# Turned rows of a graph-attention stack: seven steps of waiting instead of four, their copies on ScalarE, and one tile of a block's closing work per step

## The chip, the cores and the metric

The kernel runs on one core of a Trainium2 chip, in one launch. The metric is the device time of one execution in microseconds (us), lower is better. A core has engines that each work through their own stream of instructions: TensorE (PE) multiplies matrices, VectorE (DVE) and ScalarE (ACT) work elementwise, GpSimd (POOL) does little here, SyncE (SP) issues the DMA transfers of this kernel. A semaphore makes an instruction wait for the work of another engine or for a DMA.

## The reference, cut to what matters

Four layers run over one graph of N = 3327 nodes with 256 features and a mask `adj` (N x N). Each ends in a residual sum and a layer norm. The first is a cosine attention, the second a graph-attention (GAT) layer, the third a query-key attention. The fourth, layer 3 of the code, is where the change acts. It has a matrix product ahead and then three GAT layers one behind the other:

```python
def _gat_layer(h, adj, W, a):
    Wh = h @ W
    f1 = Wh @ a[:F_out]
    f2 = Wh @ a[F_out:]
    e = leaky_relu(f1 + f2.T, ALPHA)
    att = where(adj > 0, e, NEG_INF)
    att = softmax(att, axis=1)
    return elu(att @ Wh)
h = input @ W0
h = _gat_layer(h, adj, W1, a1)
h = _gat_layer(h, adj, W2, a2)
h = _gat_layer(h, adj, W3, a3)
...
x = _layernorm(x + h)
```

All is float32. Nearly all the arithmetic is in the products `att @ Wh`, one per layer, 3327 x 3327 by 3327 x 256.

## The kernel before

**Tiles, blocks, steps.** The nodes are padded to 26 tiles of 128. The rows of the result are worked on in seven blocks of 512 rows (four tiles), the last one, block 6, of 256. There are six layers in the code, "0", "1", "2", "3a", "3b" and "3c"; the last three are the GAT layers of layer 3, and `deep(L)` is true for them. One list of steps `(L, b, j)` runs over layers, blocks and the 26 tiles `j` of the sum. In each step the loop makes attention weights some steps ahead, issues the matmuls of the step, and then calls `advance()` once.

**Weights.** For a tile, `Gat.weights` lets ScalarE write `re` (L787) into one of four buffers and VectorE multiply it with the mask into `ft` (L800). In the deep layers two pairs of tiles are then combined on VectorE by `quad_sums` (L871 to L874), or one pair by `sums` (L883 to L886), since products go pair by pair in a Strassen form of seven products: 13 pairs a block. A pair has 14 matmuls (L935), each of them two records in the profile. The other operand of the form, sums of rows of `v`, is written to memory once by `combine` (L843 to L853) and fetched for each block and pair by `fetch_tsum` (L857, `tsums`). Blocks 0 to 5 use this form, block 6 the plain one (L1644; in 3c a form of its own, L1610).

**Closing a block.** When the last pair of a block is done, its sums stand in PSUM, and `finish(L, b, pos)` has to turn them into rows of the next layer. It is a generator: each `advance()` carries it from one `yield` to the next, so that it is spread over the steps of the next block. In the deep layers it does this: `joined` adds up the seven products (L961 to L979); `normed` divides by the row sums (L1175, L1177); `turn` transposes the four tiles; `projected` multiplies a tile with the layer's weights (L1230, `pproj`), and ScalarE takes `exp` and `relu` of it (L1239, L1242); `activated` joins these into `v` (L1254); `follow` adds to the sum of rows (L1084) and to the scores of the next layer (L719); `combine` follows each second tile. In 3c a layer norm and the store of the result follow instead.

**Turning.** `turn` lets ScalarE split the rows into their low and high 16-bit halves (`planes`, L990), issues one DMA transpose on SP (L993), waits `steps` yields, and copies the two halves from `turned` into `pT` on VectorE (L1000). How many yields it waits is said by `turn_steps` (L1003): four, but in block 5 (`NB - 2`) seven, and nine in 3c. In block 5 `finish` also yields after each `activated`.

**Order.** SP's queue holds, besides the transposes, the fetches of `tsums`, the mask of the next block (1664 KB, issued in step 8), the stores of `combine` and the rows of scores. What is left of a closing at step 22 of a block is carried out there at once. A scheduler then places the instructions of each engine, so an instruction can stand elsewhere in its engine's stream than the step in which it was issued.

Of the kernel before, what the change touches and what calls it, by code (L numbers as in the profile page):

```python
# [33 lines left out]
def gnn_stack(ctx: ExitStack, tc: tile.TileContext, a: dict, N: int, out: bass.AP):  # L34
# [8 lines left out]
    nc = tc.nc  # L43
    NT = (N + P - 1) // P
    NP = NT * P
    NB = (NP + CH - 1) // CH
# [36 lines left out]
    n = 8  # L83
# [738 lines left out]
    def deep(L):  # L822
        return L.i > 2
# [6 lines left out]
    def combine(key, p, v, e=None):  # L830


        b1, b2 = v[2 * p], v[2 * p + 1]
        b11, b12, b21, b22 = b1[:, H:D], b1[:, :H], b2[:, H:D], b2[:, :H]
        if (key, p) in kept or key == "0":
            t = work.tile([P, 4 * H + 1], F32, tag="tsum", name="tsums", bufs=3)
        else:
            t = work.tile([P, 4 * H + 1], F32, tag="x4k", name="tsum", bufs=2)
        if (key, p) in kept:
            tsums[kept[key, p], p] = t  # L840
        t1, t2, t3, t4 = (t[:, c : c + H] for c in (0, H + 1, 2 * H + 1, 3 * H + 1))
        if e is None:
            nc.gpsimd.memset(t[:, H : H + 1], 1.0)  # L843
            nc.vector.tensor_tensor(t1, b12, b11, ALU.subtract)
            nc.vector.tensor_tensor(t3, b22, b12, ALU.subtract)
        else:
            one = t[:, H : H + 1]
            nc.vector.tensor_scalar(one, e[:, :1], 0.0, None, ALU.is_ge)
            nc.vector.scalar_tensor_tensor(t1, b12, one, b11, ALU.mult, ALU.subtract)
            nc.vector.scalar_tensor_tensor(t3, b22, one, b12, ALU.mult, ALU.subtract)  # L850
        nc.vector.tensor_tensor(t2, b22, t1, ALU.subtract)
        nc.vector.tensor_tensor(t4, t2, b21, ALU.subtract)
        nc.sync.dma_start(t_d[key][p], t)  # L853
# [126 lines left out]
        return z[:, : 2 * q]  # L980


    def turn(x4, n, out, steps=3):

        half = "p k (n t) -> p t k n"
        pl = work.tile([P, 4, 2, D], U16, tag="x4k", name="planes", bufs=2)
        for t in range(2):
            nc.scalar.copy(pl[:, :n, t, :], x4[:, :n, :].bitcast(U16).rearrange(half, t=2)[:, t])  # L990
        yield
        tr = work.tile([P, 16, P], U16, tag="stage", name="turned", bufs=4)
        nc.sync.dma_start_transpose(  # L993
            out=tr[:, : 4 * n, :], in_=pl[:, :n].rearrange("p k t n -> p (k t n)")
        )
        for _ in range(steps):
            yield
        trv = tr[:, : 4 * n, :].rearrange("p (k t h) i -> p t k h i", t=2, h=2)
        for t in range(2):
            nc.vector.tensor_copy(out(t), trv[:, t])  # L1000
        yield

    def turn_steps(L, b):  # L1003

        if L.key == "1":
            return 5 if b == NB - 2 else 3
        return (9 if L.key == "3c" else 7) if b == NB - 2 else 4

# [82 lines left out]
    def finish(L, b, pos):  # L1093
# [4 lines left out]
        n = len(ts_)  # L1098
# [71 lines left out]
        else:  # L1170
# [23 lines left out]
            if L.key in x_d:  # L1194
                x4 = work.tile([P, 4, D], F32, tag="stage", name="x4", bufs=4)
# [8 lines left out]
            if L.key != "2":  # L1204
                pT4 = work.tile([P, 4, 2, P], F32, tag="x4k", name="pT4", bufs=2)
                yield from turn(
                    p4,
                    n,
                    lambda t: pT4[:, :n].bitcast(U16).rearrange(
                        "p k h (i t) -> p t k h i", t=2  # L1210
                    )[:, t],
                    turn_steps(L, b),
                )
                pTs = {k: pT4[:, k] for k in range(n)}
                if L.key == "1" and b < NB - 2:
                    c4 = work.tile([P, 4, D], F32, tag="x4k", name="c4", bufs=2)
                    yield from projected4(pT4, w[L.w], c4)

            def projected(k):


                if L.key == "2":
                    src = p4[:, k, :]
                elif L.key == "1" and b < NB - 2:
                    src = c4[:, k, :]
                else:
                    pm = bank("pproj")
                    pT = pTs.pop(k)
                    for h in range(2):
                        nc.tensor.matmul(  # L1230
                            pm[:, :D],
                            pT[:, h, :],
                            w[L.w][:, h, :],
                            start=(h == 0),
                            stop=(h == 1),
                        )
                    src = pm[:, :D]
                e = work.tile([P, D], F32, tag="elu_e", name="elu_e", bufs=2)
                nc.scalar.activation(e, src, AF.Exp)  # L1239
                if L.hidden:  # L1240
                    y = work.tile([P, D], F32, tag="y", name="z", bufs=6)
                    nc.scalar.activation(y, src, AF.Relu)  # L1242
                else:
                    y = work.tile([P, D], F32, tag="y", name="y", bufs=6)
                    nc.vector.scalar_tensor_tensor(
                        y, src, 0.0, xr[k], ALU.max, ALU.add
                    )
                es[k] = e
                ys.append(y)

            def activated(k):
                e, y = es.pop(k), ys[k]
                x = nxt[ts_[k]][:, :D] if L.hidden else y
                nc.vector.scalar_tensor_tensor(x, e, 1.0, y, ALU.min, ALU.add)  # L1254
                if L.hidden:
                    follow([k], {k: x})
                else:
                    stats(k)

            for p in range(n + 2):  # L1260
                if p >= 2:
                    activated(p - 2)
                    if b == NB - 2:
                        yield
                    if L.hidden and p % 2 and b < NB - 1:
                        combine(layers[L.i + 1].key, (ts_[0] + p - 3) // 2, nxt)
                if 1 <= p <= n:
                    projected(p - 1)
                if p > 0:
                    yield  # L1270
        if not L.hidden:
# [29 lines left out]
            if L.key == "1":  # L1301
                yield from turn(
                    o4,
                    n,
                    lambda t: FT[b].bitcast(U16).rearrange(
                        "p h (k i t) -> p t k h i", k=4, t=2
                    )[:, t, :n],
                    4 if b == NB - 2 else 3,
                )
                for k, t in enumerate(ts_):  # L1310
                    pm = bank("pv")
                    for h in range(2):
                        nc.tensor.matmul(
                            pm[:, :D],
                            FT[b][:, h, k * P : (k + 1) * P],
                            w["v"][:, h, :],
                            start=(h == 0),
                            stop=(h == 1),
                        )
                    nc.vector.tensor_tensor(nxt[t][:, :D], pm[:, :D], w["bv"], ALU.add)  # L1320
                    if k % 2:
                        yield
                        if b < NB - 1:
                            combine("2", t // 2, nxt)
                dsts = [nxt[t][:, :D] for t in ts_]
# [146 lines left out]
    steps = [(L, b, j) for L in layers for b in range(NB) for j in range(NT)]  # L1472
# [79 lines left out]
    for s, (L, b, j) in enumerate(steps):  # L1552
# [146 lines left out]
        if j == NT - 1:  # L1699
            if b == 0 and not last:  # L1700
                nl = layers[L.i + 1]
                L.sum = Sum()
                if nl.is_gat:
                    if nl.key == "1":
                        while "row_1" not in w:
                            next(setup)
                    nl.gat = Gat(nl.key)
                    L.gat_next = nl.gat
            if end:
                pending.append(finish_last(pos[1:], xm, 1))  # L1710
            else:
                pending.append(finish(L, b, pos))
            advance()
# [65 lines left out]
```

## Time and profile before

| | before |
|---|---|
| median of 3 runs | 2300.66 us (2299.2 to 2301.87) |
| the profiled execution | 2297.41 us |
| its span in the profile | 2295.6 us |
| its mean granted TensorE clock | 0.996 |
| TensorE busy | 2257.2 us (98%) |
| VectorE busy | 1998.3 us (87%) |
| ScalarE busy | 1210.3 us (53%) |
| layer 3, from about 1370 us | some 926 us of the span |

The profile is one execution as the hardware recorded it. The busy rows give each engine's share of the span; the waits view lists, for each group of waiting instructions, the engine, the operation and its line, what released it, then the total in us, the number of times and the longest; the timeline lists instructions or runs of them in order of time, with start and duration, and in brackets the idle time ahead and what ended it. In a group's line `x54` is a number of instructions and `449/738/757` the least, mean and largest duration in ns.

### The profile page before, as it was taken

How to read it: one execution, taken by the hardware profiler on the slowest of the kernel's cores; microseconds unless marked ns; L12 is line 12 of the kernel's file. 1: busy time of each engine (PE TensorE's matmuls, PEld its weight loads, DVE VectorE, ACT ScalarE, POOL GpSimd, SP SyncE). 2: the span in 40 equal slices, each digit the busy share in tenths (PEclk: the TensorE clock that was granted, in tenths of full speed). 3: DMA queues.
4: the chain of work that ended last, by engine and by line, in shares of the span. 5: the costliest groups of instructions: out<-in, count | busy, mean ns of one | idle time of the engine just before them, and what ended most of it. 6: DMA issues, size and time to landing. Idle time of an engine off the chain costs nothing. (4 is left out here: it accounts for less than half of the span.)

```text
span 2295.6 us, 41529 instructions
## 1 busy us (share of the span) xinstructions
PE 2257.2 (98%) x15183; PEld 2004.7 (87%) x15183; DVE 1998.3 (87%) x5437; ACT 1210.3 (53%) x1982; POOL 49.4 (2%) x196
## 2 busy tenths in 40 slices
PE   9999999999999999999999999999999999999997
PEld 7788888888888877888888899999999999999997
DVE  7789999866777777898898889999899999899996
ACT  4667777764555423223223246555666555655653
POOL 0000001000000000000000000000000000000000
PEclk9999999999999999999999999999999999999999
DMA  8655565523222322132132254444444445355542
GB/s 281 192 178 179 186 195 187 161 84 89 78 72 55 105 61 81 56 100 81 56 99 71 74 171 130 133 136 143 124 129 137 131 134 148 98 152 169 149 122 58
DMA packets 186207, 286.13 MB, mean 125 GB/s; under 512 B 80413, under 2 KB 105492, under 8 KB 181396
## 3 DMA queue, kind: packets, MB, share of 16 engines
q1 hardware_dynamic: 185732, 283.22, 41.2%
q8 instruction: 120, 1.97, 0.4%
q14 instruction: 83, 0.68, 0.1%
q10 hardware_dynamic: 272, 0.26, 0.0%
HBM read 228.21 MB, written 38.44 MB: 116 GB/s over the span
## 5 line engine op out<-in xcount | busy, mean ns | idle before, releaser
L787 ACT ACTIVATE re<-u,nrh,th 128x512 f32<-128x512 f32 (+1 forms) x728 | 539.8, 778 | 343.0 <-DVE ft L800 179.7
L1644 PE MATMUL po<-v,e 128*128 128x257 f32 x1872 | 422.3, 381 | 0.9 <-ACT p L1177 0.8
L1644 PEld LDWEIGHTS po<-v,e 128*128 128x128 f32 x1872 | 352.6, 190 | 60.9 <-issue 9.8
L935 PE MATMUL po<-tsums,qsum 128*128 128x128 f32 (+1 forms) x2520 | 352.8, 275 | 1.4 <-DMA tsums<-t3b_d 0.7
L800 DVE SCALAR_TENSOR_TENSOR ft<-re,rh,mask 128x512 f32<-128x512 f32 x468 | 341.1, 747 | 2.6 <-ACT re L787 2.6
L935 PEld LDWEIGHTS po<-tsums,qsum 128*128 128x128 f32 x2520 | 316.2, 192 | 3.5 <-DVE qsum L873 1.6
L935 PE MATMUL po<-tsums,ssum 128*128 128x128 f32 (+1 forms) x2082 | 293.2, 276 | 4.0 <-DMA tsums<-t3a_d 1.7
L935 PE MATMUL po<-v,ft 128*128 128x129 f32 x1872 | 286.1, 276 | 1.3 <-DVE p L975 0.6
L935 PEld LDWEIGHTS po<-tsums,ssum 128*128 128x128 f32 x2082 | 262.6, 192 | 7.0 <-DVE ssum L885 2.0
L935 PEld LDWEIGHTS po<-v,ft 128*128 128x128 f32 x1872 | 248.2, 192 | 4.0 <-issue 1.8
L935 PEld LDWEIGHTS po<-v,e 128*128 128x128 f32 x1196 | 172.3, 191 | 37.6 <-issue 24.9
L935 PE MATMUL po<-v,e 128*128 128x129 f32 x1196 | 185.1, 275 | 0.0
L800 DVE SCALAR_TENSOR_TENSOR e<-re,rh,mask 128x512 f32<-128x512 f32 (+1 forms) x234 | 149.1, 657 | 38.4 <-PE po L1644 28.4
L524 ACT ACTIVATE ex<-ps,rq 128x512 f32<-128x512 f32 (+1 forms) x183 | 118.9, 652 | 114.7 <-PE ps L511 109.9
L511 PE MATMUL ps<-ft 128*128 128x512 f32 (+1 forms) x364 | 166.9, 564 | 0.0
L496 DVE SCALAR_TENSOR_TENSOR e<-ex,mask 128x512 f32<-128x512 f32 (+1 forms) x182 | 115.8, 650 | 49.0 <-ACT ex L694 27.1
L935 PE MATMUL po<-tsums,ft 128*128 128x128 f32 x936 | 144.2, 275 | 0.0
L525 DVE SCALAR_TENSOR_TENSOR e<-ex,mask 128x512 f32<-128x512 f32 (+1 forms) x183 | 116.8, 644 | 31.1 <-ACT ex L524 30.5
L686 PE MATMUL ps<-gT,ft 128*128 128x512 f32 (+1 forms) x336 | 129.8, 527 | 0.0
L935 PE MATMUL po<-v,qsum 128*128 128x128 f32 x840 | 128.8, 275 | 0.0
L935 PEld LDWEIGHTS po<-tsums,ft 128*128 128x128 f32 x936 | 124.9, 193 | 0.3
L660 ACT ACTIVATE ex<-ex,off 128x512 f32<-128x512 f32 x98 | 67.0, 716 | 101.7 <-DVE ex L676 69.1
(346 smaller groups left out, 3572.8 us busy)
## 6 DMA issues: line engine op xcount, KB each, us to landing
mask<-mask_d SPq DMA_DIRECT2D x30, 1664.0 KB
stage<-in_adj_a SPq DMA_DIRECT2D x78, 512.0 KB
tsums<-t_d SPq DMA_DIRECT2D x152, 256.5 KB
tsums<-t3a_d SPq DMA_DIRECT2D x77, 256.5 KB
tsums<-t3b_d SPq DMA_DIRECT2D x77, 256.5 KB
tsums<-t3c_d SPq DMA_DIRECT2D x77, 256.5 KB
mask_d<-mask SPq DMA_DIRECT2D x6, 1664.0 KB
u<-s_d SPq DMA_DIRECT2D x24, 256.0 KB
```

Source lines behind the costliest of these rows:

```text
L496: nc.vector.scalar_tensor_tensor(e[:, :wd], t_[:, :wd], 0.0, mask(b, j), ALU.add, ALU.mult)
L511: nc.tensor.matmul(ps[:, :wd], FT[j // 4][:, 0, (j % 4) * P : (j % 4 + 1) * P], FT[b][:, 1, :wd], start=True, stop=True,)
L524: nc.scalar.activation(t_[:, c], ps[:, c], AF.Exp, scale=rq[:, j : j + 1])
L525: nc.vector.scalar_tensor_tensor(e[:, c], t_[:, c], 0.0, mask(b, j)[:, c], ALU.add, ALU.mult)
L660: nc.scalar.activation(x[k], x[k], AF.Exp, bias=off, scale=1.0 / D**0.5)
L686: nc.tensor.matmul(ps[:, :wd], FT[j // 4][:, h, (j % 4) * P : (j % 4 + 1) * P], g[:, h, :wd], start=(h == 0), stop=(h == 1),)
L787: nc.scalar.activation(t_[:, :wd], self.u[b][:, :wd], AF.Relu, bias=self.nrh[:, j : j + 1], scale=self.th[:, j : j + 1],)
L800: nc.vector.scalar_tensor_tensor(e[:, :wd], t_[:, :wd], self.rh[:, j : j + 1], mask(b, j), ALU.add, ALU.mult,)
L935: nc.tensor.matmul(o, x, y, start=(p == 0 and g not in banks[:i]), stop=(p == NT // 2 - 1 and g not in banks[i + 1 :]),)
L1644: nc.tensor.matmul(pos[k], e[:, k * P : (k + 1) * P], V[L.i % 2][i], start=(i == 0), stop=(i == NT - 1),)
```

## The change

Three things change in the closing of blocks. `turn` gets a parameter for the copy, and in the deep layers it is ScalarE's. `turn_steps` gives seven everywhere but in layer 1, and in block 5 of 3c nine as before. And in the deep layers the generator yields after each `activated` also in blocks 0 to 4, so that these blocks' `projected` and `activated` go on one tile per `advance` (a step has `activated` of one tile and, in the next, `projected` of another), as block 5 did before. Block 6 of 3a and 3b gets the seven steps and ScalarE's copies too, and no added yield; block 6 of 3c does not go through `finish`.

```diff
-    def turn(x4, n, out, steps=3):
+    def turn(x4, n, out, steps=3, copy=nc.vector.tensor_copy):
...
         for t in range(2):
-            nc.vector.tensor_copy(out(t), trv[:, t])
+            copy(out(t), trv[:, t])
         yield
 
     def turn_steps(L, b):
 
         if L.key == "1":
             return 5 if b == NB - 2 else 3
-        return (9 if L.key == "3c" else 7) if b == NB - 2 else 4
+        return 9 if L.key == "3c" and b == NB - 2 else 7
...
                     turn_steps(L, b),
+                    nc.scalar.copy if deep(L) else nc.vector.tensor_copy,
                 )
...
             for p in range(n + 2):
                 if p >= 2:
                     activated(p - 2)
-                    if b == NB - 2:
+                    if b == NB - 2 or deep(L) and b < NB - 1:
                         yield
                     if L.hidden and p % 2 and b < NB - 1:
                         combine(layers[L.i + 1].key, (ts_[0] + p - 3) // 2, nxt)
                 if 1 <= p <= n:
                     projected(p - 1)
                 if p > 0:
                     yield
```

Lines from 1213 on stand one further down in the changed kernel.

## The prediction

> **What bounds the kernel now.** I read the page's engine rows first. TensorE and VectorE are both nearly full, so neither can be late without the other feeling it:
>
> ```profile
> PE 2257.2 (98%) x15183; PEld 2004.7 (87%) x15183; DVE 1998.3 (87%) x5437; ACT 1210.3 (53%) x1982; POOL 49.4 (2%) x196
> ```
>
> The change acts in layer 3 alone (3a, 3b, 3c, from 1370 us on). There I asked the waits view for PE alone, from 1300 us to the end. Columns: total us, times, longest.
>
> ```profile
> PE pproj L1230 <- DVE pT L1000: 12.7, 13, 2.3
> PE po L935 <- DMA tsums<-t3a_d: 1.7, 2, 1.4
> ```
>
> All gaps of PE that the timeline shows there add up to 24.8 us; these 12.7 us are half, and 11.8 of them lie in the closings of blocks 0 to 4, the rest in those of block 5. The timeline shows how one arises (3b, closing of block 2; start, duration):
>
> ```profile
> 1823.04 0.32 SPq L857 DMA_DIRECT2D tsums<-t3b_d  x1
> ...
> 1823.45 2.99 SPq L993 DMA_TRANSPOSE turned<-planes  x1
> ...
> 1829.84 1.37 DVE L1000 COPY pT<-turned 128x1024 uint16<-128x1024 uint16 x2 [2.38 <-issue]
> ```
> ```profile
> 1831.27 4.54 PE L1230 MATMUL pproj<-w_l_w,pT 128*128 128x256 f32 x12 [2.23 <-DVE pT L1000]
> ```
>
> The transpose is issued right behind the fetch ahead of it in SP's queue, lands 6.4 us later, VectorE has stood idle 2.38 us for it, copies for 1.37 us, and PE starts the projection 2.23 us late. Fifteen such closings (blocks 0 to 4, three layers): ten transposes were copied 4.3 to 4.9 us after issue, five (3a blocks 0, 2, 3; 3b blocks 2, 3) 6.0 to 6.6. The profile does not tell why.
>
> The projections in the last fence took 4.54 us for 12 records; elsewhere 12 take 2.86. The stretches view (us, PE busy, granted clock) says why:
>
> ```profile
> 1830.00:1831.00 1.00, 0.00 (x0) 1.00 0.00 0
> 1831.00:1832.00 1.00, 0.73 (x2) 0.72 0.00 0
> 1832.00:1833.00 1.00, 1.00 (x4) 0.50 0.00 0
> ```
>
> Half clock for some 3.3 us. It came after the gaps of 2.23 and 2.30 us and not after that of 2.09. The projections of those two blocks took 5.54 and 5.42 us against 3.89: 3.2 us more. So 11.8 + 3.2 = **15.0 us** is the prize in blocks 0 to 4.
>
> **What the Trainium skill says.** "TensorE: Matmul & The Clock Gate", What's actually happening: an idle window of about 3.4 us throttles PE to half clock until it has been busy as long. The trace agrees on half and on the length, but here 2.23 us sufficed; the trace decides. The same page, Architectural detail: ScalarE and VectorE are strict FIFO, so what stands behind a waiting copy waits too; the idle 2.38 us agree. "ScalarE: Activation LUTs", What ACT_TABLE_LOAD costs: without pointer operands 186 ns + 0.833 ns an element, so 1039 ns for 1024 elements. The trace has 1039 ns for the same size the other way (planes):
>
> ```profile
> L1000 DVE COPY pT<-turned x54: 449/738/757, 520.5 to 2264.3; 128x1024 uint16<-128x1024 uint16 x48, 128x512 uint16<-128x512 uint16 x6
> ...
> L990 ACT COPY planes<-p x54: 602/1039/1046, 514.1 to 2258.3; 128x1024 uint16<-128x1024 uint16 x48, 128x512 uint16<-128x512 uint16 x6
> ```
>
> **The change, part by part.** Since a scheduler places the instructions, I counted in the built programs' instruction order.
>
> *Seven steps.* The edit moves the copies from step 5 to step 8. But the order before had the first projection not at step 6: it stood behind 74, 73, 69, 68, 65 matmuls of the next block in 3a (closings of blocks 0 to 4), 68, 67, 67, 66, 68 in 3b, 69, 66, 67, 67, 68 in 3c. After the change: 74, 70, 70, 70, 72; 70, 72, 73, 72, 72; 70 five times. A matmul is two records of 0.1115 us (eight in 0.89 us in the timeline), 0.223 us. So PE's cover grows by -0.7 to +1.6 us, not by three steps of 3.1 us a pair. The transpose gains little: it stands behind the fetch for pair 5, which PE releases; only in 3a block 1 and 3c block 1 is it now behind pair 4. It may leave 1.4 us earlier in the first, as VectorE has less backlog (3a's planes ended 9.0 to 10.4 us after the block's first product, 3b's 8.7 to 9.2), and 0.3 in 3a block 0.
>
> *Copies on ScalarE.* VectorE loses 1.36 us and the wait, per closing. On ScalarE two copies take 1.98 us (the planes pair), so PE's operand is ready 0.62 later. Behind the waiting copy stand the next weights' L787; four buffers are filled ahead, some 4 x 1.45 = 5.8 us of VectorE's work, which hides a wait of 2 us plus the copy. If ScalarE comes late instead (5 to 7 L787 stand between planes and copy: four at 0.73 us, the rest at VectorE's pace of 1.45, so 4 to 7 us), the copy begins late by up to 1 us.
>
> Gap expected = gap now + 0.62 - 0.223 x places - earlier issue. 3a: 1.25, 0.28, 2.49, 1.89, 0. 3b: 0.17, 0, 1.51, 1.58, 0.39. 3c: 0.40, 0.14, 0.24, 0.50, 0.17. Sum **11.0**; one exceeds 2.23, so 1.6 for the clock: 12.6 against 15.0, **-2.4 us**.
>
> *One tile per step.* Projections now stand 10 to 14 matmuls apart, not in one run of six to eight. Same instructions, so nothing, hidden by PE's products; the row sums' wait of 0.2 us for VectorE may go. VectorE's relief could remove other small waits: 0 to -1.5, I take **-0.5**.
>
> *Block 5's closing* (steps were seven already; copies move): 0.48 and 0.42 + 0.62 - two matmuls of 0.44: **-0.5** together. In 3c it ends the program: the PE gap of 0.97 becomes 0.97 + 0.62 - 0.45: **+0.2**.
>
> *Last block's closing* (3a to 3b, 3b to 3c) goes from place 44 to 70, the mean row's matmul from 126 to 140, the combine behind the sums for tiles 24 and 25. On SP the mask fetch (1664 KB) is in front of the next block's first fetch; PE waited 0.65 and 0.39 for that. The mask waits for tile 25's weights, now about 0.4 us later: **+0.8**; bounds 0 and +4. Other DMAs keep their number.
>
> Sum: -2.4 - 0.5 - 0.5 + 0.2 + 0.8 = **-2.4 us** on the profiled execution's 2297.41 (span 2295.6). The median of the runs is 2300.66, 3.25 above; so 2298.3.
>
> **The rivals.** *The change doesn't do what it says* is thus my forecast: seven steps are there in the source, not on PE, and the longer copy takes back what the places give. Chance 0.40, 2298.
>
> *The five late transposes land early,* as ten did (1.9 us less): their gaps shrink to 0.6 in all, the sum falls from 11.0 to 2.9 without a clock drop, 12.1 less than now: 2288. For it: landing is not tied to the copy's engine, and ten in fifteen were early. Against: the fetch behind each stays. Two or three of five give 2293. Chance 0.34.
>
> *The half clock spreads:* the five late ones come 0.6 us later still, because ScalarE reaches or ends its copy late; then all exceed 2.23 or nearly. 5 x 0.6 + 4 x 1.6 = 9.4 more: 2308, slower. It decides from a gap of some 2.2 us. For it: 1.25 to 2.5 us are expected already. Against: VectorE's freed time. Chance 0.26.
>
> **How the numbers follow.** A measurement of this kernel tells about 0.2%, 4.6 us, from no change. Forecast 2298.3; no change 0.40, faster 0.34, slower 0.26. Range 2287 to 2309 takes in both rivals; the likeliest case alone spans 2295 to 2303.
>
> **What would show it.** Right: L1000 on ACT at 1.0 us each, PE waits for it of about 11 us in all, longest near 2.5, clock halved once. Wrong: under 5 us of such waits (faster), or four halved clocks (slower), or PE waiting for quad sums.

## The result, and the profile after

The changed kernel takes **2309.2 us** (median of five runs, 2307.54 to 2311.25) beside 2299.2 us of before on the same chip (2297.95 to 2301.87). The ratio is 1.0042, with a 95% interval of 1.0027 to 1.0056: slower by 10 us. The prediction had 2298.3, no change, and a range that ended at 2309.0. The profiled execution spans 2308.6 us, 13.0 more than that of before; it is 1.3 us over its own median, and that of before 1.8 under the 2299.2, so that 3 of the 13 are scatter.

The engine rows of the page come first. VectorE is rid of 20 us, ScalarE has 43 us more, and PE, which has the same work, is as full as before:

```profile
PE 2258.1 (98%) x15183; PEld 2005.9 (87%) x15183; DVE 1978.7 (86%) x5397; ACT 1253.7 (54%) x2022; POOL 43.6 (2%) x196
```

The waits view for PE from 1300 us to the end (total us, times, longest):

```profile
PE pproj L1231 <- ACT pT L1000: 21.6, 16, 3.0
PE po L935 <- DMA tsums<-t3a_d: 3.5, 4, 1.6
PE po L935 <- DVE ft L800: 1.9, 2, 1.6
```

The wait for the turned rows is still the largest, and has grown from 12.7 to 21.6 us. What became of it is read from the groups of the two kinds of copies on ScalarE (least, median and largest duration in ns; the middle figure is a median in the prediction's lines too, not a mean):

```profile
L1000 ACT COPY pT<-turned x40: 755/1330/1355, 1437.1 to 2277.3; 128x1024 uint16<-128x1024 uint16 x36, 128x512 uint16<-128x512 uint16 x4
...
L990 ACT COPY planes<-p x54: 609/1040/1046, 514.8 to 2270.7; 128x1024 uint16<-128x1024 uint16 x48, 128x512 uint16<-128x512 uint16 x6
```

Same engine, same 1024 elements of the same type, and yet 1.330 us and not 1.040. The planes copies read every second element and write consecutive ones; the pT copies read consecutive ones and write every second. The timeline of one closing (3a, block 1) has the consequence:

```profile
1479.37 3.11 SPq L993 DMA_TRANSPOSE turned<-planes  x1
...
1486.10 2.52 ACT L1000 COPY pT<-turned 128x1024 uint16<-128x1024 uint16 x2 [3.66 <-DMA turned<-planes]
...
1488.67 2.07 PE L1231 MATMUL pproj<-w,pT 128*128 128x256 f32 x4 [3.04 <-ACT pT L1000]
```

The transpose lands late (6.73 us after issue), ScalarE has stood idle 3.66 us for it and starts at once, so it did not come late itself; its two copies take 2.52 us, where VectorE's took 1.37, and PE waits 3.04 us. PE's clock in the stretches behind it (us, PE busy, granted clock):

```profile
1487.00:1488.00 1.00, 0.00 (x0) 1.00 0.25 92
1488.00:1489.00 1.00, 0.33 (x1) 0.54 0.00 0
1489.00:1490.00 1.00, 1.00 (x3) 0.50 0.00 0
```

Three closings of 3a end so, with gaps of 2.62, 3.04 and 2.35 us, and each such drop costs 1.7 us (the missing clock, summed over its stretches). Before had three drops in layer 3 too: the two that the prediction names, and one at 1381 us, at the start of 3a, that is absent after. So the clock accounts for none of the difference in all, though for one more drop in the closings.

The gaps of PE in the timeline from 1360 us on, each counted once, add up to 20.5 us before and 32.8 after. (The prediction gives 24.8 for before; that sum held three gaps twice, since two merged rows start at the same time. So the 12.7 us are over 60% of the gaps and not half; no sum of the prediction used it.) Of the 12.3 us more, 6.6 are waits for pT in blocks 0 to 4 (11.8 to 18.4), 1.3 the closings of block 5 (1.87 to 3.18), and 4.4 small waits elsewhere: fetches of tsums 1.9, VectorE's joining (L973, L975) 1.8, weights 1.6, less 1.4 of sums that are no longer waited for, and the rest. One execution of the changed kernel does not settle the sizes: in another (e6 below, 7.2 us faster) the waits in blocks 0 to 4 are 15.2 us and not 18.4, the clock drops two and not three, the closings of block 5 the same 3.2, and the small waits elsewhere 0.9 over before and not 4.4.

### The profile page after: what moved, and what is told of

The parts are those of the page before. It is cut to its first block, busy times and chain, and to the rows that moved or that the text cites. A ratio compares the mean times of both kernels' runs of the same rounds, so it can differ in the third digit from the quotient of the medians.

```text
span 2308.6 us, 41591 instructions
## 1 busy us (share of the span) xinstructions
PE 2258.1 (98%) x15183; PEld 2005.9 (87%) x15183; DVE 1978.7 (86%) x5397; ACT 1253.7 (54%) x2022; POOL 43.6 (2%) x196
## 4 chain that ended last, share of the span: by engine, by line
PE 76%; DVE 11%; DMA 6%; ACT 6%; issue 2%; POOL 0%; ACTq 0%; DVEq 0%; POOLq 0%; SPq 0%
PE po L935 35%; PE po L1645 15%; PE ps L647 6%; PE ps L511 6%; PE ps L686 5%; DMA turned<-planes 4%; DVE ft L800 3%; PE pproj L1231 3%; ACT pT L1000 2%; ACT planes L990 1%; ACT re L787 1%; PE pv L1314 1%; ACT p L1175 1%; PE pgq L541 1%; DMA tsums<-t3a_d 1%
## 5 line engine op out<-in xcount | busy, mean ns | idle before, releaser
L935 PEld LDWEIGHTS po<-v,ft 128*128 128x128 f32 x1872 | 253.1, 193 | 9.2 <-issue 3.0
```

The source lines that it names most:

```text
L935: nc.tensor.matmul(o, x, y, start=(p == 0 and g not in banks[:i]), stop=(p == NT // 2 - 1 and g not in banks[i + 1 :]),)
```

## The experiments

The table gives for each run the ratio to before on the same chip, with its interval, PE's waits for pT, and all its listed gaps from 1360 us on, in us of one profiled execution. Two executions of the same program (changed and e6) differ by some 3 us in the third column and by 6.7 in the last, so small differences there say nothing. The third column follows the waits view: the last closing of 3c is booked there under `zlast` in most runs with VectorE's copies (1.0 us in before, 2.2 in e17) and is then not in it; with ScalarE's copies it is. In e13 to e18 the added load is that of blocks 0 to 4 of the three deep layers.

| run | ratio (95%) | pT | all gaps |
|---|---|---|---|
| before | 1 | 12.7 | 20.5 |
| changed | 1.0042 (1.0027 to 1.0056) | 21.6 | 32.8 |
| e1: changed, VectorE copies | 0.9994 (0.9986 to 1.0002) | 7.6 | 24.6 |
| e2: before, ScalarE copies | 1.0046 (1.0032 to 1.0060) | 25.4 | 32.3 |
| e3: before, seven steps | 0.9994 (0.9986 to 1.0002) | 6.3 | 22.0 |
| e4: before, nine steps | 0.9934 (0.9921 to 0.9946) | 0.9 | 16.6 |
| e5: nine steps, ScalarE copies | 0.9996 (0.9987 to 1.0004) | 3.3 | 22.1 |
| e6: changed again | 1.0038 (1.0026 to 1.0051) | 18.4 | 26.1 |
| e7: before, transposes from ScalarE's queue | 1.0017 (1.0010 to 1.0024) | 13.7 | 22.8 |
| e8: before, one tile per step | 1.0008 (1.0000 to 1.0016) | 12.3 | 23.8 |
| e9: changed, one copy for two | 1.0000 (0.9992 to 1.0008) | 15.9 | 22.5 |
| e10: before, eleven steps | 0.9925 (0.9913 to 0.9937) | 1.5 | 14.2 |
| e11: eleven steps, GpSimd copies | 1.0052 (1.0040 to 1.0065) | 0.9 | 33.5 |
| e12: eleven steps, ScalarE copies | 1.0004 (0.9996 to 1.0012) | 3.5 | 25.3 |
| e13: e4 and ScalarE's load | 0.9932 (0.9919 to 0.9944) | 0.9 | 12.5 |
| e14: e4 and ScalarE's wait | 0.9935 (0.9921 to 0.9948) | 0.9 | 13.6 |
| e15: e4 and ScalarE's time | 0.9929 (0.9916 to 0.9941) | 1.0 | 13.8 |
| e16: e5 and VectorE's load | 0.9964 (0.9952 to 0.9976) | 3.5 | 16.6 |
| e17: e1 and ScalarE's load | 1.0003 (0.9995 to 1.0011) | 6.5 | 25.6 |
| e18: changed and VectorE's load | 1.0035 (1.0023 to 1.0047) | 19.1 | 30.2 |

**e1, the copies undone.**

```diff
-                    nc.scalar.copy if deep(L) else nc.vector.tensor_copy,
```

> The changed kernel with the copies of the turned rows back on VectorE; seven steps and one tile per step stay. Theory 1 (the price of ScalarE's copies: a pair takes 2.53 us there and 1.37 on VectorE, all of it ahead of PE's first projection): the waits of PE for pT fall from 21.6 to about 7 us, each by up to 1.16, and the three halved clocks (1.7 us each) go with gaps under 2.2: 2291 to 2297. Theory 2 (the late tail of a closing: the row of scores and its store stand at matmul 154 of 182 and not at 98, so fetches of tsums and VectorE's joining come late): stays at 2304 or more. Theory 3 (transposes that land late, moved to other blocks by the new order): the same blocks stay late, five landings over 6 us, gaps only 0.6 shorter, about 2303.

2296.5 us; its waits for pT in the waits view:

```profile
PE pproj L1230 <- DVE pT L1000: 7.6, 7, 2.0
```

That is Theory 1 in size (about 7 expected) and time; Theories 2 and 3 are out as the main cause. But gaps that are not for pT are 17.0 us, beside 7.8 in before and 11.2 in the changed kernel, and one clock drop is left.

**e2, ScalarE's copies alone.** Before, with the copies of deep layers on `nc.scalar.copy`.

> The kernel before with the copies on ScalarE alone; four steps, and all tiles in one go. Theory 1: PE's waits for pT rise from 12.7 to some 20 us, as 15 x 1.16 comes on and the first projection stands 2 to 3 matmuls later on average (39 in all, 8.7 us); one or two more halved clocks: 2307 to 2313. Theory 2: nothing in the tail has moved, so within 3 us of before, 2297 to 2302.

2307.3 us, four clock drops in the closings, every closing waits:

```profile
PE pproj L1231 <- ACT pT L1000: 25.4, 18, 3.1
```

So the copies alone make the whole of the loss, with or without the other two parts.

**e3 and e8, the other two parts alone.**

```diff
e3  +        return 9 if L.key == "3c" and b == NB - 2 else 7
e8  +                    if b == NB - 2 or deep(L) and b < NB - 1:
```

> The kernel before with seven steps alone; copies on VectorE. First projections stand behind 70 to 73 matmuls (before 65 to 74), row of scores at 126. Theory 1: gaps fall by some 0.223 x 35 at most, 12.7 to about 7, and one or two halved clocks go: 2291 to 2296. Theory 2: the later row costs 1 to 2 us: no gain, 2298 to 2302.

> The kernel before with one tile per step alone; four steps, copies on VectorE. Row of scores at matmul 126 and not 98, second to fourth tile at 70 to 84. Theory 1: nothing on PE's path has moved, 2296 to 2301. Theory 2 (the late tail costs): 2302 to 2306.

e3 gave 2297.0 us beside 2298.0, at the edge between the two theories: pT's waits halve to 6.3 and no clock drop is left (5.1 us), but the other gaps rise from 7.8 to 15.7, for tsums, VectorE's joining and sums of weights. So most of what the head of the closing has won is lost elsewhere. The later tail may take it, or PE, which comes earlier, may meet other limits; e3 does not tell these apart. e8 is 1.8 us over before by the ratio, and its interval begins at 1.0000; its other gaps are 3.7 us more, at nearly the same waits for pT. Both parts together (e1) are worth nothing either.

**e4 and e10, PE really later.** Before, with nine, then eleven steps in blocks 0 to 4.

```diff
-        return (9 if L.key == "3c" else 7) if b == NB - 2 else 4
+        if b == NB - 2:
+            return 9 if L.key == "3c" else 7
+        return 9 if b < NB - 1 else 4
```

> The kernel before with nine steps in blocks 0 to 4 of layer 3 (block 5 and 6 as before), copies on VectorE. The first projection stands behind 84 matmuls and not 65 to 74, 2 to 4 us more of products to cover the landing; the row of scores at 140. Theory 1 with PE's place: no gap for pT over 0.5 us in blocks 0 to 4, their 11.8 us and the two halved clocks (3.4) go: 2284 to 2290. Theory 2: the later tail gives 5 us or more back: 2294 to 2300.

> As the run with nine steps and VectorE's copies, but eleven: first projection behind 98 matmuls (84), row of scores at 154 (140). If the cover at 84 was enough, nothing more is gained on pT (0.9 us left in all) and the later tail costs 0 to 5 us: 2281 to 2287. If late landings were still felt through VectorE's stream: 2277 to 2280.

e4 takes **2281.6 us**, 16.4 less than before, better than both kernels; e10 2281.7 beside 2298.9, the same within the intervals. In the profiled executions the listed gaps and the clock drops explain 9.0 of the 11.4 us between before and e4: the waits for pT fall by 11.8 and the drops by 5.1, and the other gaps rise by 7.9. A transpose issued at 1816.03 us in e4 lands late as ever, and VectorE copies in two pieces at 1822.67 and 1823.90, but PE comes only when all is there (PE, then VectorE, in the timeline; no bracket for PE means no wait):

```profile
1825.30 1.03 PE L1232 MATMUL pproj<-w_l_w,pT 128*128 128x256 f32 x4
...
1822.67 0.75 DVE L1000 COPY pT<-turned 128x1024 uint16<-128x1024 uint16 x1 [1.32 <-issue]
1823.90 0.75 DVE L1000 COPY pT<-turned 128x1024 uint16<-128x1024 uint16 x1
```

Seven steps left the first projection behind 70 to 75 matmuls and gained 0.06%, with an interval that takes in none; nine put it behind 84 (92, 89 and 85 in the first three closings of 3a) and gained 0.7%. What counts is its place in PE's stream, not the count of steps.

**e6 and e9, the price of the copy.** One ScalarE copy of 2048 elements for the two, writing consecutively:

```diff
+            copy(out(None), tr[:, : 4 * n, :].rearrange("p (k t h) i -> p k h i t", t=2, h=2))
```

> The changed kernel, but ScalarE copies both halves in one instruction of 2048 elements that writes consecutive 16-bit elements and reads alternately from two places, where the two copies write every second element. If the written stride is what makes 1.33 us of the 1.04 that the planes copies take (which read every second element and write consecutive ones): about 2 x 0.85 + 0.2 = 1.9 us, 0.6 less than 2.53, PE's waits for pT fall from 21.6 to 12 or 13 and the time to 2297 to 2302. If the price follows the number of elements or the reading pattern: 2.5 us or more and 2307 to 2312.

In e6 the condition in front of the new line never held, so this is the changed kernel once more: 1.0038, in agreement with 1.0042. It serves as a repeat. Of the changed kernel's five late transposes (6.07 to 6.73 us from issue to copy) the four in 3a are late again (5.99 to 6.26), the one in 3b is not (6.23, then 4.58).

> The changed kernel with one ScalarE copy of 2048 elements in layer 3 that writes consecutive 16-bit elements and reads alternately from two places (the earlier try at this left the two copies as they were, so it was the changed kernel once more). If the written stride makes the price (planes write consecutively and read every second element at 1.04 us for 1024): about 1.9 us and not 2.53, PE's waits for pT some 9 us fewer, 2299 to 2303. If the price goes with what is read or with the count: 2.5 us or more, 2305 to 2311.

```profile
L999 ACT COPY pT<-turned x20: 1153/2134/2144, 1434.1 to 2261.4; 128x2048 uint16<-128x2048 uint16 x18, 128x1024 uint16<-128x1024 uint16 x2
```

2.134 us, between the two expectations: 0.39 us less than the pair's 2.52. 18 closings make 7 us of that, and the ratio fell by 0.0042, 9.6 us, or by 8.7 from the repeat; one clock drop is left where there were three (two in the repeat). So the time answers to the length of the copy; PE's waits for pT fell by 5.7 us, or 2.5 from the repeat. Less 186 ns a copy (the Trainium skill, "ScalarE: Activation LUTs", What ACT_TABLE_LOAD costs), an element costs 1.12 ns with the spaced writes, 0.95 here and 0.83 in the planes. The page's 0.833 ns holds for the planes alone. The written stride is part of the price, unless the alternating read is itself cheaper than the consecutive one, which no run tried; what else in the pattern makes the rest was not separated.

**e5 and e12, ScalarE's copies with PE later.**

> Nine steps in blocks 0 to 4 of layer 3 and the copies on ScalarE (block 5 keeps its steps, block 6 four), all tiles in one go. Theory 1 (ScalarE's slower copy costs only what of it lies on PE's path): PE comes to the projection behind 84 matmuls, 18.8 us after the block's first product, a late landing with its 2.5 us of copying ends at about 18.5, so the copies cost nothing there and VectorE is rid of 1.4 us a closing: 2277 to 2285, like the nine steps with VectorE's copies (2281.6) or a little under. Rival (ScalarE's stream itself suffers: the next weights stand behind a copy that waits): 2289 or more.

> Eleven steps with the copies on ScalarE. PE's path has 3 us more of cover than with nine, so no wait for pT in blocks 0 to 4. Theory F: VectorE's waits for ScalarE some 30 us as with nine steps, 2291 to 2299. If the loss with nine steps came of something that more cover removes: 2286 or less.

My theory fell here. PE waits for pT in no closing of blocks 0 to 4, as it said, and yet e5 takes 2296.2 us, 14.6 more than e4, and e12 17.5 more than e10. VectorE now waits for ScalarE, in the waits view for VectorE from 1360 us on:

```profile
DVE v L1257 <- ACT z L1245: 10.9, 12, 2.5
DVE ft L800 <- ACT re L787: 9.5, 7, 2.4
DVE y L1248 <- ACT elu_e L1242: 8.2, 6, 3.9
```

In e4 these are 2.2, 2.6 and 2.7 us. So I took ScalarE's stream for the cause (theory F), and tried the copies on an engine with nothing to do.

**e11, GpSimd's copies.**

> Eleven steps and the copies of blocks 0 to 4 of layer 3 on GpSimd, which has nothing else to do there; blocks 5 and 6 keep VectorE. Theory F (ScalarE's stream: behind a copy that waits and takes 2.5 us stand the next weights and the exp and relu of the projections, for which VectorE then waits): ScalarE is free, VectorE's waits for ScalarE (z, elu_e, re) stay near the 10 us of before, and the time within 5 us of eleven steps with VectorE's copies, 2277 to 2288. Theory G (it is the schedule without VectorE's copies, or PE's place): 2292 or more as with ScalarE's copies. If a pair on GpSimd takes over 5 us, PE waits for it, and that shows as its own wait.

2310.7 us, slower than all. It could not tell F from G, since it brought a cost of its own:

```profile
L1000 POOL COPY pT<-turned x30: 1557/1784/2566, 1435.1 to 2231.6; 128x1024 uint16<-128x1024 uint16 x30
```
```profile
1435.91 1.77 DVE L800 SCALAR_TENSOR_TENSOR ft<-re,rh,mask 128x512 f32<-128x512 f32 x1
```

The `ft` in the second fence (timeline of VectorE, beside a GpSimd copy from 1435.14 to 1438.88) takes 1.77 us, where the median is 0.74. VectorE's busy time is 14 us more than e10's although 30 copies, some 22 us, have left it. The Trainium skill, "GPSIMD Engine Reference", 1. Specifications, has it that GpSimd's SBUF interface is shared with VectorE, in contention with instructions of two SBUF inputs, which `ft` is; the trace agrees for this `ft`, but the `qsum` in front of it (L873, 1435.31 us, two SBUF inputs too) kept its 0.68 us beside the same copy.

**e13, e14, e15, ScalarE's load off the path.** e4, and ScalarE makes the same copies into a dead buffer, or one element of them, or ten small copies that wait for nothing (337 ns each).

```diff
+            dead = pl[:, :n].rearrange("p k a (b i t) -> p t k (a b) i", t=2, b=1)
+            for t in range(2):
+                nc.scalar.copy(dead[:, t], old[:, t])
```

> Nine steps with VectorE's copies, and in blocks 0 to 4 of layer 3 ScalarE makes the same two copies too, after the same wait for the landing, into a buffer that nobody reads (the planes, dead by then). PE's operand comes from VectorE as in the run with nine steps (2281.6 us); ScalarE carries all that it carried with nine steps and its own copies (2296.2). If ScalarE's stream is the cause (weights, exp and relu stand behind): 2293 to 2302, VectorE's waits for ScalarE near 30 us and not 9. If the cause is VectorE's stream or the order without its copies: 2281 to 2286.

> The same, but ScalarE copies a single element a partition after the wait for the landing: the wait without the 2.5 us. If the wait in ScalarE's queue (22 us in all in the changed kernel) is what keeps weights back: 2287 to 2296. If the time of the copies does it: 2281 to 2286.

> The same, but ScalarE makes ten small copies of 192 elements from the planes instead, which wait for nothing, about 2.5 to 3 us in all: the time without the wait. If ScalarE's time does it: 2287 to 2296. If the wait is needed: 2281 to 2286.

All three are e4 again. In e13 ScalarE waits 17.7 us for landings and copies for 1.35 us twice a closing, and VectorE hardly notices:

```profile
DVE v L1262 <- ACT z L1250: 3.5, 5, 1.2
DVE y L1253 <- ACT elu_e L1247: 2.7, 2, 1.4
DVE ft L800 <- ACT re L787: 2.6, 2, 1.3
```

Theory F is out as long as VectorE makes PE's copies: neither ScalarE's time nor its wait is the cause, alone or together. The run is a clean one: the built program of e13 has the instructions of every engine in e4's order, with the added copies between them (and so has e17, below, beside e1).

**e16, e17, e18, the streams and the operand apart.** e16 and e18 leave ScalarE's operand and let VectorE make the same copies into the dead buffer; e17 is the reverse in the changed kernel.

> Nine steps with ScalarE's copies (2296.2 us without more), and in blocks 0 to 4 of layer 3 VectorE makes the same two copies too, at their place in its stream, into the dead planes. PE's operand comes from ScalarE, 1.16 us later than from VectorE; both streams carry the copies and their waits. Theory Q (the later operand is carried on: the projections' exp and relu come late, VectorE's joining and the closing's end behind them): 2290 to 2299. Theory P (without the copies VectorE runs ahead of ScalarE, its stream stands in an order in which it waits for exp and relu in front of weights that it could make): 2281 to 2287.

> The changed kernel with the copies on VectorE (2296.5 us), and in blocks 0 to 4 of layer 3 ScalarE makes the same two copies into the dead planes. With nine steps this load cost nothing. If it costs nothing with seven steps and one tile per step either: 2293 to 2300, and ScalarE's time and wait are out as causes. If it does: 2303 or more.

> The changed kernel (operand from ScalarE), and in blocks 0 to 4 of layer 3 VectorE makes the same two copies too, into the dead planes. Theory Q (PE's operand is 1.16 us later in each closing, with PE waiting already): 2305 to 2312 as changed, PE's waits for pT near 20 us. Theory P (VectorE's order without copies): 2293 to 2300.

| who feeds PE, who else copies | seven steps, one tile | nine steps |
|---|---|---|
| VectorE, nobody | 0.9994 (e1) | 0.9934 (e4) |
| VectorE, ScalarE too | 1.0003 (e17) | 0.9932 (e13) |
| ScalarE, VectorE too | 1.0035 (e18) | 0.9964 (e16) |
| ScalarE, nobody | 1.0042 (changed) | 0.9996 (e5) |

From the second row to the third the edit swaps only the source of PE's operand in blocks 0 to 4; in blocks 5 and 6 the copies move with it, and the scheduler places some other instructions anew. That is 0.32%, 7.4 us, in both columns. With seven steps it shows as PE's waits:

```profile
PE pproj L1236 <- DVE pT L1005: 6.5, 8, 1.5
```
```profile
PE pproj L1237 <- ACT pT L1005: 19.1, 15, 2.8
```

The first is e17, the second e18. In blocks 0 to 4 the waits rise from 5.6 to 16.3 us; with the last closing of 3c counted on both sides, block 5 has 3.0 and 2.8, so it is not the reason. One pair of the same closing (3a, block 2; e17, then e18):

```profile
1534.40 1.13 PE L1236 MATMUL pproj<-w,pT 128*128 128x256 f32 x4 [1.48 <-DVE pT L1005]
```
```profile
1536.44 1.13 PE L1237 MATMUL pproj<-w,pT 128*128 128x256 f32 x4 [2.77 <-ACT pT L1005]
```

In closings 0 to 3 of 3a the gaps are 1.45, 0.95, 1.48 and 1.28 us in e17 and 2.32, 1.94, 2.77 and 2.32 in e18, about the 1.16 us that the operand is later each time, and in the built programs the first projections stand within one matmul of the same place. The rest of the column, ScalarE's load and VectorE without its copies, is 0.09% and 0.07%, not to be told from nothing. So in the changed kernel **the later operand is the cause**. But the other gaps fall by 5.9 us in return, so that all listed gaps rise by 4.6 only. With nine steps the last row costs another 0.32%: VectorE without copies of its own does worse than with dead ones, and its waits for z, elu_e and re fall from 31.9 us to 16.8 when the dead ones are put back. In the built programs PE's order is nearly the same in e16 and e5, while about 1000 of VectorE's 5374 instructions stand in other places. That the waits come of this order is likely, but was not tried by itself. How the swap costs 7.4 us with nine steps stays open too: PE waits for pT there for 0.5 us in one closing of 3a, block 5 has 0.9 us more than in e13, and in e16 the first three closings of 3a project 8, 5 and 1 matmuls earlier than in e13. So PE's waits need not be the only way in which the swap costs time with seven steps either.

**e7, the late landings.**

```diff
-        nc.sync.dma_start_transpose(
+        (nc.scalar if steps > 3 and n == 4 else nc.sync).dma_start_transpose(
```

> The kernel before with the transposes of four tiles issued by ScalarE's queue, straight behind the planes, and not by SyncE's, where they stand behind a fetch of tsums and hold up the next one for 3 us. If late landings (6.0 to 6.8 us and not 4.3 to 4.9) come of sharing SyncE's queue with the fetches: none late, PE's waits for pT fall from 12.7 to about 4 us, 2286 to 2293. If they come of the DMA engines' load whoever issues: as many late, 2295 to 2302. If the issue holds ScalarE's stream for 1.5 to 3 us, weights come late and it is slower: 2303 or more. Layers 1's transposes of four tiles with more than three steps (its block 5) are moved too.

2301.5 us, 0.17% over before. Six of 15 copies in blocks 0 to 4 start 6.2 us or more after the issue, one of them 7.8: sharing SyncE's queue is not what makes them late. The issue does hold ScalarE's stream (queue and engine, from the timeline); in 17 of the 18 issues from 1360 us on the next weights start 0.04 to 0.05 us after its end, here too, although the view names an `ft`:

```profile
1430.16 3.03 ACTq L993 DMA_TRANSPOSE turned<-planes  x1
1433.24 2.93 ACT L787 ACTIVATE re<-u,nrh,th 128x512 f32<-128x512 f32 x4 [2.39 <-DVE ft L800]
```

Why some transposes land 1.8 us late stays open.

## Why the prediction was wrong, point by point

**What bounds** was right: PE, with its waits for pT as the largest single loss. e4 took nearly all of them away, and the two clock drops behind them, and won 16.4 us against the 15.0 of the prize. But the other gaps, 7.8 us in before, were 15.7 then, so they are no fixed sum.

**Seven steps** were right in mechanism. That they do not move the projection by three steps was read from the order, and e3 gives 0.06%.

**The copies on ScalarE** are the step that failed: "On ScalarE two copies take 1.98 us (the planes pair), so PE's operand is ready 0.62 later." The pair takes 2.52 us, so it is 1.16 later, and 0.54 us in each of 15 closings, at most 8.1 in all, are missing. Put into the prediction's own formula closing by closing (two of them stood at nothing with cover to spare), it gives 18.3 us of gaps; 18.4 were measured, 15.2 in the repeat. That the sum fits so well is luck in part: the formula takes the late transposes to be the same five, and has 3.0 us for 3a block 2, where PE waited for nothing, and nothing for block 4, where it waited 2.0. I had taken the nearest row of the trace and the price of the Trainium skill that agreed with it ("ScalarE: Activation LUTs", What ACT_TABLE_LOAD costs), and called the two directions alike. The row's copy writes consecutively, the new one does not, and no upper bound for that was carried into the range.

**The clock** follows from it: one drop was expected in those closings (1.6), three came (5.1). With the gaps that is 23.5 against a forecast of 12.6, 10.9 us more. The whole account, for the two profiled executions: they differ by +13.0 where -2.4 was forecast, 15.4 us; 10.9 come from here, 1.6 from block 5, 4.1 from the small waits, and the drop at 1381 us that is absent takes 1.7 off, which leaves 0.5. That the median, too, lies 10.9 above the forecast is chance: the medians differ by +10.0, 12.4 over the -2.4.

**Cover on ScalarE**, "four buffers are filled ahead": VectorE's waits for ScalarE (z, elu_e, re) rose from 10.1 us to 31.6, those for re alone from 4.5 to 11.2, so the cover failed as stated. It cost next to nothing: e18 has 12.4 us less of these waits than the changed kernel and 0.07% less time.

**Block 5** was put at -0.5 and +0.2. Its gaps grew by 1.3; the three pairs' missing 0.54 us each are 1.6, on a forecast of -0.3, so the same term accounts for it.

**One tile per step** at nothing holds within the measurement (e8). The relief of VectorE at -0.5 did not show: the other small waits rose by 4.4, or by 0.9 in the repeat. e8, with VectorE's copies, has 3.7 more as well, so they may come with the later tail and need not come of the copies; at a scatter of some 3 us this is not shown. Of the last block's 0.8, 0.45 came: PE waits 1.10 us for 3b's first fetch, and for 3c's no longer, but 0.53 for VectorE's joining there.

**The rivals.** The third, 2308, hit the time. Its start was true, copies that end late, but by their length and not because ScalarE reached them late, and by 0.54 us in all closings and not 0.6 in five; two of its five clock drops did not come. The second, late transposes that land early, did not happen: five were late again, in partly other blocks.

## What to carry to other kernels

Before a copy is moved to another engine, price it by a row with the same strides on the side that it writes, not by the same number of elements, and carry the dearer end into the range where no such row is there. An operand that PE already waits for gets no cover from relief elsewhere: here VectorE, freed of 20 us, won nothing, while one pair of products more in front of the waiting matmul (nine steps) won 0.7%. And read from the order where the waiting instruction stands, since three steps more in the source moved it only from behind 65 to 74 matmuls to behind 70 to 75, and the next two by a whole pair.

## What the runs showed of the hardware that was not expected

- ScalarE copies 1024 16-bit elements in 1.040 us when it reads every second and writes consecutively, in 1.330 us the other way; VectorE takes 0.738 us for the latter, GpSimd 1.784.
- A GpSimd copy can hold a VectorE instruction with two SBUF inputs for a whole microsecond (1.77 us for 0.74).
- Length alone does not tell whether a gap of PE halves the clock. A gap of 1.88 us did (e8), 1.93 (e1) and 2.03 (e5) did; 2.09 (before) and 2.77 (e18) did not, and of two gaps of 2.32 us in e18 one did and one did not. So the prediction's limit of some 2.2 us does not hold. The Trainium skill, "TensorE: Matmul & The Clock Gate", What's actually happening, says that activity is watched in a free-running window of about 3.4 us. With that a gap's place in the window would count as well as its length, which would go with two equal gaps that end differently; but all of these gaps are shorter than the window, so its rule that a whole idle window halves the clock does not give them, and no run shows where the windows lie.
- The issue of a transpose of four tiles in layer 3 holds the queue that issues it, SyncE's for 1.5 to 3.3 us (changed) and ScalarE's for 1.7 to 3.1 (e7).
